# A decoder layer whose attention reads keys, queries and values from DRAM in padded rows

## The chip, the cores and the metric

The kernel runs on one core of one Trainium2 chip. The metric is the device time of one execution in microseconds (us); what is compared is the median of several executions. A profile is one execution taken by the hardware profiler. Its engines are PE (matmuls; their weight loads are listed apart as PEld), DVE, ACT and POOL (vector, scalar and general engines), and SP, which here only issues DMAs. "L702" is line 702 of the kernel before unless it is said to be of the kernel after.

## The reference, cut to what matters

x is 4 batches of 512 tokens of 256 features, float32. Three blocks follow one another, each with a residual:

```
x = x + mamba(layernorm(x))                 # two layers of a selective state space (SSM)
x = x + attention(layernorm(x), ctx_1024)   # 16 heads of 16, keys and values from ctx_1024
x = x + ffn(layernorm(x))                   # shared MLP and 8 experts, the best 2 of a token
```

The middle one is the one that the change is about:

```
q = h @ Wq.T + bq;  k = ctx @ Wk.T + bk;  v = ctx @ Wv.T + bv      # 4 batches, 512 x 256
p = softmax((q / 4) k^T)  per head of 16
return (p v) @ Wo.T + bo
```

A row of p sums to one, so bv adds the same vector to every row of p v, and bv @ Wo.T can be added to bo instead.

## The kernel before, in words

**SSM.** There are 8 steps (layer, batch), of 40 units each, in one loop over `units`. A unit with n > 0 treats one state of 256 channels over 512 tokens, as tiles of 128x1024: POOL multiplies m (L645), DVE scans v (L680) and h (L689), POOL multiplies h with Cs (L702), PE sums over the states into y (L716). Units with n = 0 come in halves of 128x512, whose first scan is done by PE as a product with a band (vf, L662). The order on every engine is the order in which the program is written. Besides its own work, a unit draws from two generators: `background`, which is the preparation of the next step (`prologue`), and `projections`, the output projection of the step before (po, L746, then the adds to the state xs and, in the second layer, of the layer's input, L755 and L757). In the last step nothing follows, and `background` is `kept_from`, which makes keys, values and queries for the attention: per batch it loads the context cT into one buffer, makes the queries of batches 0 to 2 (`queries`), the keys (pk, L820) and the values (pv, L841, with the bias bv as a matmul of a row of ones), and stores all three to DRAM as they are: 256 rows of 512. A line at the end of the unit decides whether `background` is advanced once or twice. When the loop ends, what is left of `kept_from` runs, then the last unit's sums, the gate z, and the last projection, that of batch 3.

**Start.** Before the loop the first step is prepared: projections (pp, L341), the short convolution (pc, L452, with the diagonal weights `taps` that POOL and others fill), dbc, rows of B and C that go through DRAM, ACT's w, ln and w (L539 to L544) in rotating buffers of one each, sums over time on PE (L524), and the copies of deltas and dxs that POOL's m needs.

**Attention.** Between the loop and the attention stand constants of the router and the loads of wg, wo, w1 (`up`), w2 (`dn`) and bo. Then the attention's own tiles are made: `kpad` and `qpad` have 4 groups of 4 heads, each head 32 partitions, of which 16 carry data; `fetched(b)` loads the data rows with 8 DMAs of 16 partitions x 4 x 512, and the rows between were filled once (zeros; in kpad a row of ones at 16, against which q carries the negative row maximum). `vpad` has 32 columns a head, 16 of them data, and a one. `fetched(b)` also loads v into a buffer, from which POOL copies it into vpad (L1251), and adds bo to the batch's state on POOL (L1252).

The attention has 16 units (batch, group) of 8 slots, again written out in order. PE works on scores twice: sc (L1329), whose row maxima DVE takes (L1335), and ten slots later (`LEAD`) sT with the maxima turned into q (`flipped`), which ACT exponentiates (L1340) and PE multiplies with vpad (L1278). sc and sT rotate through three PSUM buffers. The first ten slots hold only sc. Between the scores one generator, `between`, is advanced by a piece per slot: first the queries of batch 3, later `projected(b - 1)` (pn, pb and po on PE, L1203 adding po to xs on DVE) and `routed(b - 1)`, which chooses experts and ends in eight scatters issued by POOL (L1133). Where the third slot of a new batch is reached, all that is left of `between` is written out at once before the next one starts. The last batch's `projected` and `routed` run with the FFN, which needs them.

Of the kernel before, what the change touches and what calls it, by code (L numbers as in the profile page):

```python
# [17 lines left out]
P = 128  # L18
# [14 lines left out]
HS = 32  # L33
# [34 lines left out]
def decoder_layer(  # L68
# [73 lines left out]


    kept = ctx.enter_context(tc.tile_pool(name="kept", bufs=1, space=bass.MemoryType.DRAM))
    kept_k = [kept.tile([D, L], F32, name=f"kept_k{b}") for b in range(B)]
    kept_q = [kept.tile([D, L], F32, name=f"kept_q{b}") for b in range(B)]
    kept_v = [kept.tile([L, D], F32, name=f"kept_v{b}") for b in range(B)]

# [4 lines left out]
    def queries(b, bank, new, wqs, bqs):  # L153
# [27 lines left out]
        for m in range(KD):  # L181
# [7 lines left out]
            yield False  # L189
        nc.sync.dma_start(blocks(kept_q[b]), qs)  # L190
        yield False

    def chained(*steps):
        for s in steps:
            yield from s


    with ExitStack() as ph:
# [57 lines left out]
        def powers():  # L256
# [18 lines left out]
            nc.vector.memset(far[:NQ, 1], 0.0)  # L275

        def banded():

            for c in range(NCH):
                w = CHUNKS[c + 1] - CHUNKS[c]  # L280
                for r in range(NQ):
                    nc.scalar.activation(
                        band[:CR, c, r, :w], power[:CR, min(c, 1), :w], AF.Copy, scale=firsts[:CR, c, r : r + 1]
                    )
                yield
# [23 lines left out]
        def load_others(l):  # L309
            outw = wp.tile([P, NE, D], F32, name="outw")  # L310
# [279 lines left out]
        def gates_of(s):  # L590
            l, b = s
            if made[s][0] is None:
                made[s][0] = [pre2.tile([P, 2, L], F32, name="z") for _ in range(2)]
            return made[s][0]
# [53 lines left out]
        ys = {}  # L648
        projections = []

        filtering = {}
# [72 lines left out]
        def finished(s, e):  # L724

            l, b = s
            z = made[s][0]
            gated = z[e // 2][:, e % 2, :]
            nc.vector.tensor_tensor(gated, ys.pop((s, e)), gated, ALU.mult)
            if e < NE - 1:  # L730
                return
            made.pop(s)
            projections.append(projected(s, z))

# [31 lines left out]
        powers()  # L766
        load_others(0)
        while pairs[1] not in stored:
            next(background)
# [16 lines left out]
        def kept_from():  # L786
# [11 lines left out]
            nc.sync.dma_start(wv, blocks(wvT))  # L798
            vs = room[:, 2 * D : 6 * D].rearrange("p (t d) -> p t d", t=TB)
            bvs = room[:1, 6 * D : 7 * D]  # L800
            nc.sync.dma_start(bvs, bv.unsqueeze(0))
            ones = room[:1, 7 * D : 7 * D + P]
            nc.vector.memset(ones, 1.0)
            where = {"xn": "big", "xnT": "u", "qs": "w"}
            for b in range(B):
                cT = pre1.tile([P, KD, L], F32, tag="ln", name="cT")
                nc.sync.dma_start(cT, blocks(ctxT[b]))
                if b < B - 1:
# [8 lines left out]
                for m in range(KD):  # L817
# [10 lines left out]
                    nc.scalar.activation(ks[:, m, :], pk, AF.Identity, bias=bks[:, m : m + 1])  # L828
                nc.sync.dma_start(blocks(kept_k[b]), ks)
                for t in range(0, TB, 2):  # L830
                    pv = ps.tile([P, 2, D], F32, tag="mm", name="pv")
                    for i in range(2):
                        for k in range(KD):
                            nc.tensor.matmul(
                                pv[:, i, :],
                                cT[:, k, (t + i) * P : (t + i + 1) * P],
                                wv[:, k, :],
                                start=(k == 0),
                                stop=False,
                            )  # L840
                        nc.tensor.matmul(pv[:, i, :], ones, bvs, start=False, stop=True)  # L841
                    yield
                    nc.scalar.copy(vs[:, t : t + 2, :], pv)
                nc.sync.dma_start(blocks(kept_v[b]), vs)

        for u, (i, n, js) in enumerate(units):
# [87 lines left out]
        finished(*pairs[-1][:2])  # L934
        for _ in projections.pop():
            pass

# [5 lines left out]
    wgs = route.tile([P, KD, NX], F32, name="wgs")  # L943
    nc.sync.dma_start(wgs, blocks(wg))
    ties_to = route.tile([P, NX, NX], F32, name="ties_to")
# [51 lines left out]
    def behind(reader, writers):  # L997
# [17 lines left out]
    nc.vector.memset(counts[0], 0.0)  # L1015


    unit_row = route.tile([P, 1], F32, name="unit_row")
    nc.vector.tensor_reduce(
        unit_row, ident.rearrange("p (j r) -> p j r", r=HS)[:, :, HD : HD + 1].rearrange("p j o -> p o j"), AX.X, ALU.add  # L1020
    )

# [142 lines left out]
    wo = att_w.tile([P, KD, D], F32, name="wo")  # L1165
    nc.sync.dma_start(wo, blocks(woT))

    up = att_w.tile([P, KD, FF], F32, name="up")
    nc.sync.dma_start(up, blocks(w1))
    dn = att_w.tile([P, NF, D], F32, name="dn")  # L1170
    nc.sync.dma_start(dn, blocks(w2))
    bos = att_w.tile([P, D], F32, name="bos")
    nc.sync.dma_start(bos, bo.partition_broadcast(P))

# [31 lines left out]
    with ExitStack() as ph:  # L1206
# [5 lines left out]
        ph.enter_context(tc.manual_schedule())  # L1212

        qpads, kpads, vpads, tops = [], [], [], []
        for i in range(2):
            q = wp.tile([P, NG, L], F32, name=f"qpad{i}")
            nc.gpsimd.memset(q, 0.0)
            qpads.append(q)  # L1220
            k = wp.tile([P, NG, L], F32, name=f"kpad{i}")
            nc.vector.tensor_copy(
                k.rearrange("p g l -> p (g l)"), unit_row.to_broadcast([P, NG * L])
            )
            kpads.append(k)
        for i in range(2):
# [3 lines left out]
            tops.append(t)  # L1230

            v = wp.tile([P, TB, NH, HS], F32, name=f"vpad{i}")
            nc.vector.memset(v, 0.0)
            nc.gpsimd.memset(v[:, :, :, HD : HD + 1], 1.0)
            vpads.append(v)
# [6 lines left out]
        def fetched(b):  # L1242

            k, q = kpads[b % 2], qpads[b % 2]
            for dst, src in ((k, kept_k[b]), (q, kept_q[b])):
                rows = src.rearrange("(g j r) t -> j r g t", j=P // HS, r=HD)
                for j in range(P // HS):
                    nc.sync.dma_start(dst[j * HS : j * HS + HD], rows[j])
            v = ring.tile([P, TB, NH, HD], F32, tag="wide", name="v")
            nc.sync.dma_start(v.rearrange("p t h d -> p t (h d)"), blocks(kept_v[b]))  # L1250
            nc.gpsimd.tensor_copy(vpads[b % 2][:, :, :, :HD], v)  # L1251
            nc.gpsimd.tensor_tensor(  # L1252
                xs[:, b], xs[:, b], bos.unsqueeze(1).to_broadcast([P, TB, D]), ALU.add
            )

# [29 lines left out]

        fetched(0)
        held = None
        between = queries(B - 1, bank, lambda shape, name: ring.tile(shape, F32, tag="wide", name=name), wqs, bqs)
        un, outs, at = {}, {}, {}
        n = B * NG * 8  # L1290
        for s in range(-LEAD, n + 2):
# [3 lines left out]
            if k == 2 and g == 0 and 0 <= b < B:  # L1295
                un[b] = att_act.tile([P, NG, L], F32, name="un")
                if b > 0:
                    for _ in between:
                        held = None
                    between = chained(projected(b - 1, un[b - 1], bank), routed(b - 1, bank))  # L1300
            if k == 2 and g == 1 and b + 1 < B:
# [41 lines left out]

            if k == 6 and u + 1 < B * NG:
                held = flipped(u + 1)
# [14 lines left out]
        for _ in between:  # L1360
            pass


    with ExitStack() as ph:
        hold = ph.enter_context(tc.tile_pool(name="ffn_hold", bufs=1))
        act2 = ph.enter_context(tc.tile_pool(name="ffn_act2", bufs=2))
        act3 = ph.enter_context(tc.tile_pool(name="ffn_act3", bufs=3))
        act6 = ph.enter_context(tc.tile_pool(name="ffn_act6", bufs=6))
# [168 lines left out]
        def combined(b):  # L1537

            for c in range(TOP):
                first = NB * P + (c * B + b) * L  # L1540
                yt = act3.tile([P, TB, D], F32, name="yt")
                came = nc.sync.dma_start(yt, blocks(rows_out[first : first + L, :]))
# [16 lines left out]
def _arranged(i):  # L1559
# [28 lines left out]
        "wvT": i[c + "Wv"].T,  # L1588
        "bv": i[c + "bv"],
        "woT": i[c + "Wo"].T,  # L1590
# [24 lines left out]
```

## Time and profile before

| | |
|---|---|
| median of 3 runs | 1897.0 us (1896.61 to 1900.17) |
| profiled execution | 1896.35 us |
| its span, first to last instruction | 1894.7 us |
| mean granted clock of PE | 0.923 |
| busy: PE, DVE, ACT, POOL | 1619.6, 1388.7, 1045.4, 1245.6 us |
| SSM: last product of POOL ends | 1271.46 us |
| first sT of the attention | 1337.90 us |
| attention's last scatters, batch 2 | 1636.95 to 1646.99 us |
| L702 and L645 on POOL (192 each) | 2357 and 2358 ns |
| L680 and L689 on DVE (192 each) | 2281 and 2287 ns |

The times of the last rows are read from timelines and the chain of waits: an instruction's start and length in us from the span's start. The chain lists the work that ended last, piece by piece in order of time, each piece being what released the next; "issue" is time in which an engine waited for nothing that the profile shows. A waits line reads: engine and line that waited, what released it, then the sum in us, how often, and the longest. In a table by stretches, a pair such as 25.69 (x198) is an engine's busy time and its number of instructions there. The granted clock is the share of full speed that PE was given.

### The profile page before, as it was taken

The numbers are of one execution on the slowest core, as the hardware profiler recorded it, in microseconds if no ns is written. First come the engines' busy times: TensorE is split into PE (matmuls) and PEld (weight loads), VectorE is DVE, ScalarE is ACT, GpSimd is POOL, SyncE is SP. The second block draws the span as 40 slices with busy tenths as digits, with TensorE's granted clock in tenths as the row PEclk, the third lists the DMA queues.
The fourth block names the chain that finished last, engine by engine and source line by source line (L and its number), as shares of the span: only waits on it lengthen the run. The fifth ranks groups of instructions, "written<-read, shape, count | busy, mean of one in ns | idle before, by whom it ended". The sixth has DMA issues, their size and how long they took to land.

```text
span 1894.7 us, 28242 instructions
## 1 busy us (share of the span) xinstructions
PE 1619.6 (85%) x10714; PEld 751.3 (40%) x10714; DVE 1388.7 (73%) x1256; ACT 1045.4 (55%) x1635; POOL 1245.6 (66%) x782
## 2 busy tenths in 40 slices
PE   7779799799789889879879888785999999899995
PEld 2333343343343343334333343333333333466663
DVE  1388899889899889899898889975466676442223
ACT  3747668658677667667686765430454444412220
POOL 3488899899899889889889989972000201244540
PEclk9689899899889889899899899986899999999997
DMA  2433434435443343532543353414220200432214
GB/s 65 113 101 105 126 90 106 123 71 120 118 115 98 105 124 90 119 111 69 140 119 82 100 126 97 138 49 100 45 34 1 56 1 23 135 122 65 64 54 136
DMA packets 116120, 173.12 MB, mean 91 GB/s; under 512 B 18737, under 2 KB 57522, under 8 KB 115986
## 3 DMA queue, kind: packets, MB, share of 16 engines
q1 hardware_dynamic: 110706, 156.86, 32.0%
q0 software_dynamic: 5280, 14.46, 2.4%
q8 instruction: 85, 1.39, 0.3%
q14 instruction: 49, 0.40, 0.1%
HBM read 118.09 MB, written 53.17 MB: 90 GB/s over the span
## 4 chain that ended last, share of the span: by engine, by line
PE 52%; DVE 14%; ACT 12%; POOL 9%; issue 7%; DMA 5%; SPq 1%; POOLq 0%; DVEq 0%; ACTq 0%; another core or an unknown queue 0%
PE y L716 6%; PE sT L1329 5%; DVE v L680 5%; PE vf L662 4%; POOL h L702 4%; PE pc L452 4%; PE pw L1508 4%; PE pu L1485 4%; DVE h L689 3%; ACT decay L636 3%; PE o L1278 3%; PE pp L341 3%; PE sc L1329 3%; POOL m L645 2%; PE sum L524 2%
## 5 line engine op out<-in xcount | busy, mean ns | idle before, releaser
L702 POOL TENSOR_TENSOR h<-h,Cs 128x1024 f32<-128x1024 f32 x192 | 452.5, 2357 | 70.0 <-DVE h L689 61.7
L645 POOL TENSOR_TENSOR m<-dxs,Bs 128x1024 f32<-128x1024 f32 x192 | 452.6, 2358 | 23.8 <-DMA dxs<-wide 23.8
L689 DVE TENSOR_TENSOR_SCAN h<-decay,v 128x1024 f32<-128x1024 f32 x192 | 439.1, 2287 | 16.6 <-ACT decay L636 0.5
L680 DVE TENSOR_TENSOR_SCAN v<-beta,m 128x1024 f32<-128x1024 f32 x192 | 437.9, 2281 | 16.8 <-POOL m L645 12.7
L636 ACT ACTIVATE decay<-deltas,scaleA 128x511 f32<-128x511 f32 x512 | 333.1, 711 | 46.2 <-DVE h L689 38.2
L716 PE MATMUL y<-h,joined 128*32 128x512 f32 x768 | 218.0, 649 | 64.8 <-POOL h L702 64.8
L1335 DVE TENSOR_REDUCE tops<-sc 128x2 f32<-128x1024 f32 x128 | 156.4, 1225 | 103.9 <-PE sc L1329 96.8
L662 PE MATMUL vf<-band,dxT 106*32 106x102 f32 (+1 forms) x5120 | 188.4, 265 | 22.1 <-DVE hh L677 21.3
L1340 ACT ACTIVATE at<-sT 128x1024 f32<-128x1024 f32 x128 | 128.7, 1024 | 127.4 <-PE sc L1329 90.2
L677 DVE TENSOR_TENSOR_SCAN hh<-decay,vf 128x512 f32<-128x512 f32 x128 | 154.0, 1203 | 55.1 <-PE vf L662 42.8
L702 POOL TENSOR_TENSOR hh<-hh,Cs 128x512 f32<-128x512 f32 x128 | 163.4, 1276 | 43.2 <-DVE hh L677 40.7
L662 PEld LDWEIGHTS vf<-band,dxT 106*32 106x32 f32 (+1 forms) x5120 | 146.8, 114 | 104.6 <-issue 79.5
L1329 PE MATMUL sc<-kpad,qpad 32*128 32x512 f32 x512 | 149.7, 684 | 22.3 <-DMA qpad<-kept_q 17.0
L341 PE MATMUL pp<-xnT,inw 128*128 128x512 f32 x256 | 132.6, 649 | 6.2 <-ACT xnT L434 3.5
L1329 PE MATMUL sT<-q,kpad 32*128 32x512 f32 x512 | 135.9, 644 | 0.0
L452 PE MATMUL pc<-xpad,taps 128*128 128x512 f32 x256 | 118.6, 604 | 4.5 <-ACT xpad L446 4.5
L716 PEld LDWEIGHTS y<-h,joined 128*32 128x32 f32 x768 | 32.8, 114 | 161.7 <-POOL h L702 97.1
L113 POOL TENSOR_TENSOR rstd<-ve,neghalf 128x4 f32<-128x4 f32 x12 | 12.3, 1027 | 121.2 <-DVE ve L111 121.2
L636 ACT ACT_TABLE_LOAD x67 | 86.0, 1283 | 10.7 <-DVE h L689 9.3
L1517 POOL DMA_INDIRECT rows_out<-yg,target x39 | 40.0, 1027 | 75.8 <-DVE xgT L1478 64.8
L1133 POOL DMA_INDIRECT rows_in<-row,at x32 | 31.8, 993 | 81.2 <-DVE hit L1150 23.2
L341 PEld LDWEIGHTS pp<-xnT,inw 128*128 128x128 f32 x256 | 47.9, 202 | 79.5 <-issue 61.7
(249 smaller groups left out, 2359.5 us busy)
## 6 DMA issues: line engine op xcount, KB each, us to landing
deltas<-wide SPq DMA_DIRECT2D x256, 128.0 KB
dxs<-wide SPq DMA_DIRECT2D x256, 128.0 KB
rows_in<-nothing SPq DMA_DIRECT2D x17, 1028.0 KB
Cs<-rows SPq DMA_DIRECT2D x128, 64.0 KB
wide<-ln SPq DMA_DIRECT2D x16, 512.0 KB
wide<-w SPq DMA_DIRECT2D x16, 512.0 KB
Bs<-rows SPq DMA_DIRECT2D x32, 192.0 KB
xt<-in_x_dram SPq DMA_DIRECT2D x8, 512.0 KB
```

Source lines behind the costliest of these rows:

```text
L341: nc.tensor.matmul(pp, weights[l][1][half][:, k, m * P : (m + 1) * P], xnT[:, k, :], start=(k == 0), stop=(k == KD - 1),)
L452: nc.tensor.matmul(pcs[j], taps[:, e, k, :], xpads[j][:, k : k + L], start=(k == 0), stop=(k == KC - 1),)
L636: nc.scalar.activation(dA[:, j, 1:], copies[i][0][:, j, 1:], AF.Exp, scale=weights[s[0]][6][:, e, q + j, n : n + 1])
L645: nc.gpsimd.tensor_tensor(m, copies[i][1], Bs[:, n - 1, :].unsqueeze(1).to_broadcast([P, 2, L]), ALU.mult)
L662: nc.tensor.matmul(v[r * QP : (r + 1) * QP, CHUNKS[c] : CHUNKS[c + 1]], made[s][5][e // 2][:k, c, first : first + QP], band[:k, c, r, : CH ...
L677: nc.vector.tensor_tensor_scan(h, dA[:, 0, :], v, 0.0, ALU.mult, ALU.add)
L680: nc.vector.tensor_tensor_scan(v.rearrange("p n t -> p (n t)"), beta.rearrange("p n t -> p (n t)"), entering.pop(u).rearrange("p n t -> p ...
L689: nc.vector.tensor_tensor_scan(h.rearrange("p n t -> p (n t)"), dA.rearrange("p n t -> p (n t)"), v.rearrange("p n t -> p (n t)"), 0.0, AL ...
L702: nc.gpsimd.tensor_tensor(h, h, Cs[n].unsqueeze(1).to_broadcast([P, len(js), L]), ALU.mult)
L716: nc.tensor.matmul(ys[s, e][(q + j) * QP : (q + j + 1) * QP, :], joined, hcs[j], start=False, stop=(u % per == per - 1),)
L1329: nc.tensor.matmul(o, l, m, start=True, stop=True)
L1335: nc.vector.tensor_reduce(top[:, t2, 2 * h : 2 * h + 2, HD : HD + 1], sc, AX.X, ALU.max, negate=True)
```

## The change

- In DRAM, keys and queries now have the padded layout: 512 rows of 512, with 32 rows a head; values have 512 columns. `rows_between`, called before the first step's preparation goes on, fills a tile of 16 partitions with zeros and one row of ones, and writes it by 8 DMAs of 512 KB (16 heads x 16 rows x 512) into the rows between of every table. The tile has the buffer that ACT's first w takes later.
- A store of keys or queries becomes two DMAs (`to_heads`). Values are put by ACT into padded buffers (three in turn, filled once by POOL) and stored by four DMAs of 256 KB a batch.
- The matmul that added bv is gone; `biased` makes bv @ Wo.T beside the scores and adds it to bos. xs + bos is now written where a new batch begins, after what was left of `between`, and for batch 3 after the attention's loop.
- In the attention, the fills and the copy into vpad are gone, and `fetched(b)` is 8 DMAs of 128x512 and one of 1 MB. `fetched(0)` comes first; the weights of attention, router and FFN are loaded after it.
- The contexts cT are loaded two ahead, and in the last step of the SSM `background` is advanced twice in every unit with n > 0.
- The last step's projection is no longer run at the SSM's end: `completed` does it as the first piece of `between`. z and outw lie in pools that live on, and the FFN's yt takes their room.
- A `flipped(-1)` that the loop ran before the first unit, and whose result nothing used, is left out.

The core of the diff:

```diff
+        def rows_between():
+
+            blank = pre1.tile([P, 2, L], F32, tag="w", name="blank")
+            nc.gpsimd.memset(blank[:HD], 0.0)
+            nc.gpsimd.memset(blank[:1, 0, :], 1.0)
+            for i, tables in enumerate((kept_k, kept_q)):
+                for dst in tables:
+                    nc.sync.dma_start(
+                        dst.rearrange("(h r) t -> r h t", r=HS)[HD:],
+                        blank[:HD, i, :].unsqueeze(1).to_broadcast([HD, NH, L]),
+                    )
...
+    def to_heads(dst, src):
+
+        for m in range(KD):
+            n = P // HD
+            rows = dst[m * n * HS : (m + 1) * n * HS, :].rearrange("(h r) t -> h r t", r=HS)
+            nc.sync.dma_start(rows[:, :HD, :], src[:, m, :])
...
         load_others(0)
+        rows_between()
...
-                        nc.tensor.matmul(pv[:, i, :], ones, bvs, start=False, stop=True)
                     yield
-                    nc.scalar.copy(vs[:, t : t + 2, :], pv)
-                nc.sync.dma_start(blocks(kept_v[b]), vs)
+                    for i in range(2):
+                        at = vs[:, (b * TB + t + i) % 3]
+                        nc.scalar.copy(at[:, :, :HD], pv[:, i, :].rearrange("p (h d) -> p h d", d=HD))
+                        nc.sync.dma_start(
+                            kept_v[b][(t + i) * P : (t + i + 1) * P, :], at.rearrange("p h r -> p (h r)")
+                        )
+                if b + 2 < B:
+                    context(b + 2)
...
-                    n > 0 and (k == 0 and slot < 20 or units[(u + 1) % len(units)][1] > 0) or slot in (8, 23, 38)
+                    n > 0 and (k == 0 and slot < 20 or k == len(steps) - 1 or units[(u + 1) % len(units)][1] > 0) or slot in (8, 23, 38)
...
         finished(*pairs[-1][:2])
-        for _ in projections.pop():
-            pass
...
+        def fetched(b):
+
+            for g in range(NG):
+                for dst, src in ((kpads[b % 2], kept_k[b]), (qpads[b % 2], kept_q[b])):
+                    nc.sync.dma_start(dst[:, g, :], src[g * P : (g + 1) * P, :])
+            nc.sync.dma_start(vpads[b % 2].rearrange("p t h d -> p t (h d)"), blocks(kept_v[b]))
...
+        between = chained(
+            completed(),
+            queries(B - 1, bank, lambda shape, name: ring.tile(shape, F32, tag="wide", name=name), wqs, bqs),
+            biased(),
+        )
...
                 if b > 0:
                     for _ in between:
                         held = None
+                    nc.gpsimd.tensor_tensor(
+                        xs[:, b - 1], xs[:, b - 1], bos.unsqueeze(1).to_broadcast([P, TB, D]), ALU.add
+                    )
                     between = chained(projected(b - 1, un[b - 1], bank), routed(b - 1, bank))
...
         for _ in between:
             pass
+        nc.gpsimd.tensor_tensor(xs[:, B - 1], xs[:, B - 1], bos.unsqueeze(1).to_broadcast([P, TB, D]), ALU.add)
```

The two new functions of the attention:

```python
        def completed():

            z, outw = left
            cur = xs[:, B - 1]
            for t in range(TB):
                po = bank("po")
                for k in range(NE):
                    nc.tensor.matmul(
                        po[:, :D],
                        z[k // 2][:, k % 2, t * P : (t + 1) * P],
                        outw[:, k, :],
                        start=(k == 0),
                        stop=(k == NE - 1),
                    )
                yield True
                nc.vector.tensor_tensor(cur[:, t, :], cur[:, t, :], po[:, :D], ALU.add)
                if t == TB - 1:
                    nc.gpsimd.tensor_tensor(cur, cur, xt, ALU.add)
                yield False

        def biased():

            wide = ring.tile([P, KD, P], F32, name="wide_bv")
            nc.scalar.copy(wide, bvs.unsqueeze(2).to_broadcast([P, KD, P]))
            pb = bank("pb")
            for k in range(KD):
                nc.tensor.matmul(pb[:, :D], wide[:, k, :], wo[:, k, :], start=(k == 0), stop=(k == KD - 1))
            yield True
            nc.vector.tensor_tensor(bos, bos, pb[:, :D], ALU.add)
            yield False
```

More of the change, by code (lines that the diff above doesn't have):

```diff
@@ L144, in decoder_layer @@
     kept = ctx.enter_context(tc.tile_pool(name="kept", bufs=1, space=bass.MemoryType.DRAM))
-    kept_k = [kept.tile([D, L], F32, name=f"kept_k{b}") for b in range(B)]
-    kept_q = [kept.tile([D, L], F32, name=f"kept_q{b}") for b in range(B)]
-    kept_v = [kept.tile([L, D], F32, name=f"kept_v{b}") for b in range(B)]
+    kept_k = [kept.tile([NH * HS, L], F32, name=f"kept_k{b}") for b in range(B)]
+    kept_q = [kept.tile([NH * HS, L], F32, name=f"kept_q{b}") for b in range(B)]
+    kept_v = [kept.tile([L, NH * HS], F32, name=f"kept_v{b}") for b in range(B)]
+    def to_heads(dst, src):
[3 more added lines that the diff above has]
+            nc.sync.dma_start(rows[:, :HD, :], src[:, m, :])
     rows_in = kept.tile([NX * ROWS + SPARE * P, RW], F32, name="rows_in")
@@ L189, in queries @@
             yield False
-        nc.sync.dma_start(blocks(kept_q[b]), qs)
+        to_heads(kept_q[b], qs)
         yield False
@@ L195, in chained @@
             yield from s
+    late = ctx.enter_context(tc.tile_pool(name="late", bufs=1))
+    late2 = ctx.enter_context(tc.tile_pool(name="late2", bufs=2))
     with ExitStack() as ph:
@@ L309, in load_others @@
         def load_others(l):
-            outw = wp.tile([P, NE, D], F32, name="outw")
+            outw = late.tile([P, NE, D], F32, name="outw")
             nc.sync.dma_start(outw, blocks(out_wT[l]))
@@ L592, in gates_of @@
             if made[s][0] is None:
-                made[s][0] = [pre2.tile([P, 2, L], F32, name="z") for _ in range(2)]
+                made[s][0] = [late2.tile([P, 2, L], F32, name="z") for _ in range(2)]
             return made[s][0]
@@ L649, in decoder_layer @@
         projections = []
+        left = []
         filtering = {}
@@ L732, in finished @@
             made.pop(s)
-            projections.append(projected(s, z))
+            if s == steps[-1]:
+                left.extend((z, weights[l][5][0]))
+            else:
+                projections.append(projected(s, z))
         def projected(s, z):
@@ L798, in kept_from, with context @@
             nc.sync.dma_start(wv, blocks(wvT))
[L799 to L803, printed above, removed]
-            where = {"xn": "big", "xnT": "u", "qs": "w"}
+            vs = room[:, KD * D :].rearrange("p (i h r) -> p i h r", i=3, r=HS)
+            nc.gpsimd.memset(vs, 0.0)
+            nc.gpsimd.memset(vs[:, :, :, HD : HD + 1], 1.0)
+            where = {"xn": "big", "xnT": "u", "qs": "w"}
+            cTs = []
+            def context(b):
+                pool, tag = ((pre1, "ln"), (pre2, "Bs"), (pre1, "ln"), (pre2, "dxT"))[b]
+                cTs.append(pool.tile([P, KD, L], F32, tag=tag, name="cT"))
+                nc.sync.dma_start(cTs[b], blocks(ctxT[b]))
+            context(0)
+            context(1)
             for b in range(B):
-                cT = pre1.tile([P, KD, L], F32, tag="ln", name="cT")
-                nc.sync.dma_start(cT, blocks(ctxT[b]))
+                cT = cTs[b]
                 if b < B - 1:
@@ L828, in kept_from @@
                     nc.scalar.activation(ks[:, m, :], pk, AF.Identity, bias=bks[:, m : m + 1])
-                nc.sync.dma_start(blocks(kept_k[b]), ks)
+                to_heads(kept_k[b], ks)
                 for t in range(0, TB, 2):
@@ L838, in kept_from @@
                                 start=(k == 0),
-                                stop=False,
+                                stop=(k == KD - 1),
                             )
-                        nc.tensor.matmul(pv[:, i, :], ones, bvs, start=False, stop=True)
                     yield
-                    nc.scalar.copy(vs[:, t : t + 2, :], pv)
-                nc.sync.dma_start(blocks(kept_v[b]), vs)
+                    for i in range(2):
[6 more added lines that the diff above has]
+                    context(b + 2)
         for u, (i, n, js) in enumerate(units):
@@ L943, in decoder_layer @@
     wgs = route.tile([P, KD, NX], F32, name="wgs")
-    nc.sync.dma_start(wgs, blocks(wg))
     ties_to = route.tile([P, NX, NX], F32, name="ties_to")
@@ L1015, in decoder_layer @@
     nc.vector.memset(counts[0], 0.0)
[L1018 to L1021, printed above, removed]
     def routed(b, bank):
@@ L1165, in decoder_layer @@
     wo = att_w.tile([P, KD, D], F32, name="wo")
-    nc.sync.dma_start(wo, blocks(woT))
     up = att_w.tile([P, KD, FF], F32, name="up")
-    nc.sync.dma_start(up, blocks(w1))
     dn = att_w.tile([P, NF, D], F32, name="dn")
-    nc.sync.dma_start(dn, blocks(w2))
     bos = att_w.tile([P, D], F32, name="bos")
-    nc.sync.dma_start(bos, bo.partition_broadcast(P))
     def projected(b, un, bank, ts=range(TB)):
@@ L1212, in decoder_layer @@
         ph.enter_context(tc.manual_schedule())
[L1216 to L1225, printed above, removed]
+        qpads = [wp.tile([P, NG, L], F32, name=f"qpad{i}") for i in range(2)]
+        kpads = [wp.tile([P, NG, L], F32, name=f"kpad{i}") for i in range(2)]
+        vpads = [wp.tile([P, TB, NH, HS], F32, name=f"vpad{i}") for i in range(2)]
+        def fetched(b):
[3 more added lines that the diff above has]
+            nc.sync.dma_start(vpads[b % 2].rearrange("p t h d -> p t (h d)"), blocks(kept_v[b]))
+        fetched(0)
+        tops = []
         for i in range(2):
@@ L1230, in decoder_layer @@
             tops.append(t)
[L1232 to L1235, printed above, removed]
+        bvs = wp.tile([P, KD], F32, name="bvs")
+        nc.sync.dma_start(bvs, bv)
         wqs = wp.tile([P, KD, D], F32, name="wqs")
@@ L1239, in decoder_layer @@
         nc.sync.dma_start(bqs, bq)
-        nc.scalar.mul(bqs, bqs, QSCALE)
[L1242 to L1254, printed above, removed]
+        xt = ring.tile([P, TB, D], F32, tag="wide", name="xt")
+        nc.sync.dma_start(xt, blocks(x[B - 1]))
+        nc.sync.dma_start(wo, blocks(woT))
+        nc.sync.dma_start(bos, bo.partition_broadcast(P))
+        nc.sync.dma_start(wgs, blocks(wg))
+        nc.sync.dma_start(up, blocks(w1))
+        nc.sync.dma_start(dn, blocks(w2))
+        nc.scalar.mul(bqs, bqs, QSCALE)
         def bank(name):
@@ L1284, in values @@
                 )
-        fetched(0)
-        held = None
-        between = queries(B - 1, bank, lambda shape, name: ring.tile(shape, F32, tag="wide", name=name), wqs, bqs)
+        def completed():
+            z, outw = left
+            cur = xs[:, B - 1]
+            for t in range(TB):
+                po = bank("po")
+                for k in range(NE):
+                    nc.tensor.matmul(
+                        po[:, :D],
+                        z[k // 2][:, k % 2, t * P : (t + 1) * P],
+                        outw[:, k, :],
+                        start=(k == 0),
+                        stop=(k == NE - 1),
+                    )
+                yield True
+                nc.vector.tensor_tensor(cur[:, t, :], cur[:, t, :], po[:, :D], ALU.add)
+                if t == TB - 1:
+                    nc.gpsimd.tensor_tensor(cur, cur, xt, ALU.add)
+                yield False
+        def biased():
+            wide = ring.tile([P, KD, P], F32, name="wide_bv")
+            nc.scalar.copy(wide, bvs.unsqueeze(2).to_broadcast([P, KD, P]))
+            pb = bank("pb")
+            for k in range(KD):
+                nc.tensor.matmul(pb[:, :D], wide[:, k, :], wo[:, k, :], start=(k == 0), stop=(k == KD - 1))
+            yield True
+            nc.vector.tensor_tensor(bos, bos, pb[:, :D], ALU.add)
+            yield False
+        held = None
+        between = chained(
[3 more added lines that the diff above has]
+        )
         un, outs, at = {}, {}, {}
@@ L1299, in decoder_layer @@
                         held = None
+                    nc.gpsimd.tensor_tensor(
+                        xs[:, b - 1], xs[:, b - 1], bos.unsqueeze(1).to_broadcast([P, TB, D]), ALU.add
+                    )
                     between = chained(projected(b - 1, un[b - 1], bank), routed(b - 1, bank))
@@ L1341, in decoder_layer @@
                 at[u, kb, h] = a
-            if k == 6 and u + 1 < B * NG:
+            if k == 6 and 0 <= u + 1 < B * NG:
                 held = flipped(u + 1)
@@ L1366, in decoder_layer @@
         act2 = ph.enter_context(tc.tile_pool(name="ffn_act2", bufs=2))
-        act3 = ph.enter_context(tc.tile_pool(name="ffn_act3", bufs=3))
         act6 = ph.enter_context(tc.tile_pool(name="ffn_act6", bufs=6))
@@ L1540, in combined @@
                 first = NB * P + (c * B + b) * L
-                yt = act3.tile([P, TB, D], F32, name="yt")
+                pool, tag = ((late2, "z"), (late2, "z"), (late, "outw"))[(2 * b + c) % 3]
+                yt = pool.tile([P, TB, D], F32, tag=tag, name="yt")
                 came = nc.sync.dma_start(yt, blocks(rows_out[first : first + L, :]))
@@ L1588, in _arranged @@
         "wvT": i[c + "Wv"].T,
-        "bv": i[c + "bv"],
+        "bv": i[c + "bv"].reshape(-1, P).T,
         "woT": i[c + "Wo"].T,
```

## The prediction

> **What bounds the kernel now.** I read the page's busy table, slices and chain first; then, for each place the change touches, a table of busy time by stretches, the chain of waits, the waits by what ended them, and single-engine timelines.
>
> The stretches (columns: length, then busy time of PE, PE's loads, DVE, ACT, POOL, then granted clock, DMA share, GB/s):
>
> ```profile
> 1145.00:1175.00 30.00, 25.69 (x198) 10.23 (x202) 28.28 (x16) 19.29 (x27) 30.00 (x16) 0.89 0.27 74
> 1285.00:1310.00 25.00, 8.00 (x36) 6.54 (x35) 12.38 (x11) 0.52 (x2) 9.20 (x18) 0.71 0.71 162
> 1310.00:1337.00 27.00, 22.27 (x60) 8.70 (x58) 15.15 (x22) 3.24 (x6) 4.59 (x4) 0.50 0.05 12
> 1400.00:1500.00 100.00, 96.58 (x602) 34.65 (x602) 69.30 (x109) 47.47 (x54) 14.81 (x16) 0.98 0.25 43
> ```
>
> The recurrence (to 1271.5) is bound by POOL with DVE behind it, the attention (1337.9 to 1636) by PE; between them lies a transition in which nothing is full. Its chain:
>
> ```profile
> 1295.48 5.24 DMA dn<-in_w_dram
> ...
> 1300.79 8.36 DMA qpad<-kept_q
> 1309.14 0.30 issue
> 1309.45 4.21 PE sc L1329 x8
> ...
> 1334.12 3.78 PE pq L184 x4
> 1337.90 1.15 PE sT L1329 x2
> ```
>
> POOL's last product of the recurrence (L702) ends at 1271.46; call it H. To the first sT (the first scores of the attention proper) it is 1337.90 − 1271.46 = 66.4 us. The padded fetches are queued on SP behind the FFN's weights, and the waits say what that costs: PE's first score waits 17.0 us for qpad.
>
> ```profile
> PE sc L1329 <- DMA qpad<-kept_q: 17.0, 1, 17.0
> ```
>
> **Transition: gain.** In the changed kernel the fetches stand first on SP. kpad's first transfer waits for H, since its room is the recurrence's; the first score then needs two of 256 KB. A cT of the same 512 KB takes 4.66 us in the chain, so the first score is near H + 4.7. The prologue from first score to first sT took 1337.90 − 1309.45 = 28.45. It loses a useless pt and q (about 1.9); the state's last projection joins it (32 records, 7.17 us at L746, before one add on POOL of 2.4), but some steps of the last batch's queries, among them the 3.78 us of pq just ahead of the first sT, slide behind it. I keep 28.5: first sT at H + 33.2, a gain of 33.2 (bounds H + 28, H + 36).
>
> Given back inside the PE-bound part: the transposes of xn (8, about 1.0), a pq (1.9), the bias product (0.9), and about 2.5 for DVE, where the normalisation stands in order ahead of score maxima and waits for x and POOL. Together 6. Net gain 27 (22 to 32). [...]
>
> **Start: the blank rows.** Eight transfers of 512 KB (4.19 MB) leave 16 partitions for DRAM. POOL fills them after its seed (12.67) and DVE's scan (15.0), so data flows from 17.5. Ahead of 41.7 the queue is empty. What is behind: rows<-dbc (41.70) in SP's queue, and ACT's w at L539 (48.09), which takes the blank's room and so waits for all eight. No 16-partition read is in the trace; the nearest row is the padded fetch, whose 128 KB pieces go into 16 partitions each:
>
> ```profile
> 1298.00:1299.00 1.00, 0.00 (x0) 0.00 (x0) 1.00 (x1) 0.00 (x0) 1.00 (x1) 0.50 1.01 349
> 1346.00:1347.00 1.00, 1.00 (x12) 0.16 (x10) 1.00 (x2) 0.98 (x1) 0.00 (x0) 1.00 1.06 107
> 1348.00:1349.00 1.00, 1.00 (x8) 0.19 (x2) 0.73 (x1) 0.87 (x1) 0.00 (x0) 1.00 1.10 107
> ```
>
> All DMA engines are busy in all three, but 16 partitions get 107 GB/s where 128 get 349. [...] At 107, 4.19 MB need 39.2 us: to about 57. At the 305 GB/s of the early loads, 14 us: to 31.5, before anyone waits. I take the row. Then w starts at 57.4 instead of 48.09, and its chain (two exponent steps, sums, DVE's w at 55.96, wide, deltas, first m at 67.0) is late by 9.3, plus cold sums: **+11** (0 to 15). Once late, POOL's first m is late by as much and the recurrence moves whole. POOL's band taps behind the fill (+3.9) end before PE needs them.
>
> **Recurrence's last step.** POOL has no room (30.00 of 30), so the fill of the padded v buffers (128x1536, near 1.8) is paid. The 32 bias matmuls leave (−7.4 of PE), batch 3's keys and values (+8, formerly 1271 to 1284) move in ahead of H, and two background steps a unit stand in front of y and vf on PE. PE has about 3.3 us spare in 30. ACT's 16 small copies and the doubled v stores (1 MB against 0.5 at 74 GB/s) fit. **+4** (0 to 9).
>
> **Attention: a wait added.** x + bos now is POOL's, queued where the batch turns. There the eight scatters of the batch before have just been given to POOL, and DVE's first `xs += po` (L1203) waits for the sum. At the last turn:
>
> ```profile
> 1636.95 1.07 POOL L1133 DMA_INDIRECT rows_in<-row,at  x1 [16.83 <-DVE hit L1151]
> ...
> 1646.01 0.98 POOL L1133 DMA_INDIRECT rows_in<-row,at  x1 [0.30 <-issue]
> ```
>
> ```profile
> 1640.04 0.42 DVE L1203 TENSOR_TENSOR xs<-xs,po 128x256 f32<-128x256 f32 x1 [1.35 <-PE po L1201]
> ```
>
> The sum would end at 1646.99 + 2.36 = 1649.4; so the add moves from 1640.04 by **+9.3**, and L1203 lies on the chain to the FFN. Behind it on DVE wait the other tokens' adds and the normalisation. For batch 2 the scatters end at 1498.97, the sum would at 1501.3, the add was at 1496.98: DVE stalls 4.4, and PE soon after, since its scores rotate through three pairs that DVE's maxima free: 3 (0 to 4.4). For batch 3, 1576.98 + 2.35 against 1574.16, 5.2 of DVE, 3 (0 to 5.2). Batch 1 finds POOL idle: 0. Sum **+15**.
>
> Padded fetches are larger afterwards (3 MB a batch against 1.5) but come as full partitions and half a batch (37 us) ahead: 0. The dropped fills, v copies and memsets lay in the transition or beside PE: already in the 33. FFN's borrowed buffers keep their number: 0.
>
> **Sum.** −27 + 11 + 4 + 15 = +3 (rounding up for joints, +4). Against the profiled 1896.35 (span 1894.7) that gives 1900; the median is 1897.0, 0.65 above, so 1901.
>
> **Rivals.**
> 1. *The blank rows are free* (reading from 16 partitions isn't held as writing into them): 11 less, 1890, faster. For: no row shows a read, and the queue is empty to 41.7. Against: the fetch row. 0.2.
> 2. *The moved work fills the last step and the prologue:* recurrence +9, first sT at H + 36, net gain 22: 1901 + 5 + 5 = 1911. For: DVE 28.28 and POOL 30.00 of 30. It decides once batch 3's keys come later than H. 0.2.
> 3. *The scatters cover nothing:* DVE's stall is caught up in batches 2 and 3 (DVE is busy only 69.30 of 100), and the last one overlaps FFN matmuls: −8 to −15, 1888 to 1893, faster. Against: L1203 at 1640.90 and 1647.01 is on the chain. 0.12.
> 4. *The change does less than it says:* the fetch is still late, since H frees its room; first score at H + 12: 1908. 0.05.
>
> **Numbers.** The likeliest case, 0.43, gives 1901 with about ±6. A measurement tells 0.2% (3.8 us) from no change: faster below 1893.2, slower above 1900.8. Case 1 and 3 give faster 0.29; the rest is split by the sum's small excess: same 0.21, slower 0.50. For 8 in 10 the range reaches to case 1's and 2's outer parts: 1885 to 1914. Faster and slower hold most; the likeliest's own range is 1895 to 1907.
>
> **What would show it.** ACT's w (L539 before) starting near 57 behind the blank DMAs, with 107 GB/s from 17 to 57, and first m near 78; if w starts at 48, case 1. H later than 1271.5 by about 15. First sc about 5 us after H, first sT about 33 after. A POOL wait of 4 to 9 us in front of the first `xs += po` in batches 2, 3 and after the attention; no such wait is case 3. I am wrong if H moves by over 20, or if the prologue runs at full clock.

## The result and the profile after

The changed kernel takes 1904.97 us (median of 10 runs, 1901.1 to 1910.88), the one before 1898.4 (10 runs): ratio 1.0038, 95% interval 1.0020 to 1.0056, or +6.6 us where +4 was forecast. The profiled execution of after is the slowest of its ten (1910.88, span 1909.2), so its end is 14.5 us later than that of before, more than the medians. Part of that is its own: between the first units and the fourth step its recurrence falls back by 5 us, which the experiment with early sums, the same up to that point, does not show. Why it falls back is open. POOL's last product of the recurrence therefore ends 22.8 us later than in before (1294.28), in the experiment with early sums 17.05 later. The ledger below uses that experiment up to there.

The start. Two stretches of after (columns as in the prediction: length, busy time of PE, PE's loads, DVE, ACT, POOL, then granted clock, DMA share, GB/s), then ACT's steps from u to w:

```profile
22.00:27.00 5.00, 5.00 (x13) 2.21 (x12) 0.00 (x0) 0.78 (x2) 5.00 (x9) 1.00 0.91 98
52.00:57.00 5.00, 0.00 (x0) 0.00 (x0) 0.00 (x0) 0.00 (x0) 0.00 (x0) 0.56 0.92 99
```

```profile
46.85 1.06 ACT L543 ACTIVATE u<-u 128x1024 f32<-128x1024 f32 x1
61.39 1.06 ACT L563 ACTIVATE w<-u 128x1024 f32<-128x1024 f32 x1 [13.48 <-issue]
```

All engines stand at 52 to 57 while the blank rows go out at 99 GB/s; w starts 13.3 later than in before (48.09). The 13.48 is labelled "issue", that is, the view names no releaser; experiments 1 and 4 tell what it was.

The transition, in after's chain:

```profile
1291.94 2.35 POOL h L727
1294.29 0.02 issue
1294.30 0.32 SPq L1249
1294.62 0.05 issue
1294.67 3.28 DMA qpad<-kept_q
1297.95 0.09 issue
1298.04 2.09 PE sc L1384 x8
...
1320.11 1.97 issue
1322.08 1.22 PE sT L1384 x2
```

The first score comes 3.8 us after POOL's last product, the first sT 27.8 after; it was 66.4. The stretch from first score to first sT, the prologue, has a mean clock of 0.78, where 1310 to 1337 of before had 0.50. The second row is a part of it, with half of the last projection's products:

```profile
1298.00:1322.00 24.00, 19.44 (x76) 9.77 (x76) 15.77 (x25) 0.20 (x1) 2.36 (x2) 0.78 0.57 194
1305.00:1315.00 10.00, 8.68 (x45) 4.43 (x45) 6.13 (x8) 0.20 (x1) 2.34 (x1) 1.00 0.68 224
```

The added wait, from the groups of after (the add of po to xs on DVE; behind the second bar the idle time ahead of it and its releasers) and from POOL's timeline:

```profile
L1230 DVE TENSOR_TENSOR xs<-xs,po 128x256 f32<-128x256 f32 x16 | 6.5, 414 | 24.1 <-POOL xs L1417 10.4 <-POOL xs L1352 9.7 <-PE po L1228 4.0
```

```profile
1490.10 0.97 POOL L1164 DMA_INDIRECT rows_in<-row,at  x1 [0.30 <-issue]
1491.08 2.36 POOL L1352 TENSOR_TENSOR xs<-xs,bos 128x1024 f32<-128x1024 f32 x1
```

In before, no POOL wait stands ahead of that add (4.9 us for PE's po). The sum follows the last scatter without a gap, and three adds of DVE wait 20.1 us for it.

### The profile page after: what moved, and what is told of

Read it like the earlier page. It is cut to its first block, busy times and chain, and to the rows that moved or that the text cites. A ratio compares the mean times of both kernels' runs of the same rounds, so it can differ in the third digit from the quotient of the medians.

```text
span 1909.2 us, 28260 instructions
## 1 busy us (share of the span) xinstructions
PE 1617.0 (85%) x10682; PEld 752.9 (39%) x10682; DVE 1380.0 (72%) x1252; ACT 1045.1 (55%) x1644; POOL 1238.1 (65%) x777
## 5 line engine op out<-in xcount | busy, mean ns | idle before, releaser
L727 POOL TENSOR_TENSOR h<-h,Cs 128x1024 f32<-128x1024 f32 x192 | 452.0, 2354 | 72.4 <-DVE h L714 66.4
L705 DVE TENSOR_TENSOR_SCAN v<-beta,m 128x1024 f32<-128x1024 f32 x192 | 437.9, 2281 | 16.5 <-POOL m L669 12.5
L113 POOL TENSOR_TENSOR rstd<-ve,neghalf 128x4 f32<-128x4 f32 x12 | 12.3, 1026 | 209.7 <-DVE ve L111 209.7
```

Of the source, the lines that this page charges most:

```text
L705: nc.vector.tensor_tensor_scan(v.rearrange("p n t -> p (n t)"), beta.rearrange("p n t -> p (n t)"), entering.pop(u).rearrange("p n t -> p ...
L727: nc.gpsimd.tensor_tensor(h, h, Cs[n].unsqueeze(1).to_broadcast([P, len(js), L]), ALU.mult)
```

## The experiments

Each ratio is to the kernel before on the same chip and in the same hours; chips differ by up to 0.3% (medians of before from 1893.14 to 1898.4), so times of different chips are compared by their ratios.

**1. Wide blank rows.** The tile has 128 partitions, a one in every 16th of its first half, and each table gets two DMAs:

```diff
-                        dst.rearrange("(h r) t -> r h t", r=HS)[HD:],
-                        blank[:HD, i, :].unsqueeze(1).to_broadcast([HD, NH, L]),
+                            rows.rearrange("(h r) t -> h r t", r=HS)[:, HD:, :], blank[:, i, :]
```

> The changed kernel with one thing different: the blank rows leave 128 partitions (16 DMAs of 256 KB) instead of 16 (8 of 512 KB); same bytes, same place in the order, same room. Port theory: 4.19 MB move at some 300 GB/s, done by about 32 us, so ACT's first w starts at 48 again (it was 61.4), the first product on POOL at 67 (it was 82), and the time falls by 15 (13 to 20) against the changed kernel, to about 1890. Rival, bytes or DRAM writes are the limit, not the partitions: the blanks still end near 60 and the time stays at 1905. Rival, the start isn't on the path: w moves back but the time falls by under 5.

Measured: 1886.89, ratio 0.9967 (0.9955 to 0.9979), 0.71% below the changed kernel's 1.0038, some 13.5 us. w starts at once after u:

```profile
45.71 1.06 ACT L548 ACTIVATE u<-u 128x1024 f32<-128x1024 f32 x1
46.85 1.06 ACT L568 ACTIVATE w<-u 128x1024 f32<-128x1024 f32 x1
```

So the slow blank rows are the price of the start. The rate was not the expected one, though: 205 GB/s at a DMA share of 0.53, not some 300. What the expectation calls the port theory rests here on the prediction's rows alone, 107 GB/s for 16 partitions and 349 for 128; no run shows ports.

```profile
28.00:32.00 4.00, 4.00 (x11) 1.78 (x10) 0.00 (x0) 0.88 (x2) 0.00 (x0) 1.00 0.53 205
```

**2. Early sums.** At the turn to batch 1 POOL adds bos to all four batches; the later sums are gone:

```diff
+                    for b2 in range(B) if b == 1 else ():
+                        nc.gpsimd.tensor_tensor(
+                            xs[:, b2], xs[:, b2], bos.unsqueeze(1).to_broadcast([P, TB, D]), ALU.add
+                        )
```

> The changed kernel with one thing different: POOL's sums xs + bos of all four batches are written at the turn to batch 1, where POOL is idle, instead of each at the turn that needs it, behind the eight scatters. Scatter theory: DVE's waits for POOL of 9.7 in the attention and 10.4 after it go, the steps from the second q on lose their jumps of 6.0, 4.9 and 8.5, and the time falls by 16 to 20 against the changed kernel, to about 1887. Rival, the jumps come from the larger fetches (3 MB a batch): only the 8.5 after the loop goes, to about 1896. Rival, PE's slack and the FFN cover it: no change, 1905.

Measured: 1883.33, ratio 0.9951 (0.9937 to 0.9965), some 16.5 us below the changed kernel. The waits for POOL are gone:

```profile
L1230 DVE TENSOR_TENSOR xs<-xs,po 128x256 f32<-128x256 f32 x16 | 6.6, 413 | 5.4 <-PE po L1228 4.5 <-issue 0.9
```

At the turn to batch 2, from the q of its first unit to the next q, it takes 22.1 us here (1466.38 to 1488.51), 22.05 in before and 28.06 in after; at the turn to batch 3 it is 22.1, 22.2 and 27.0. The fetches are as large as in the changed kernel, so they are not what made the jumps.

**3. Both** (version 3 from here on).

> Both edits together: wide blank rows and the early sums. If the two costs are separate, they add: 15 + 18 = 33 less than the changed kernel, 1872 (1866 to 1878), faster than the kernel before by over 1%. If they share a wait, the sum falls short of the two single gains by several us.

Measured: 1865.58, ratio 0.9863 (0.9846 to 0.9881), and again, beside experiments 8 and 9, 1865.59, ratio 0.9859 (0.9838 to 0.9880). Below the changed kernel by 33 us, where the two single gains make 30. By the intervals the two agree: the costs are separate. This is the fastest version: 1.4% faster than before.

> The version with both edits once more, as the measure for the next two on the same chip: ratio to before 0.986 (0.984 to 0.989), and the transition as it was: first score 3 to 5 us after POOL's last product, first sT 27.7 after.

**4. A room of its own for the blank tile**, one of h's buffers, which nothing else needs until the first unit:

```diff
-            blank = pre1.tile([P, 2, L], F32, tag="w", name="blank")
+            blank = ring3.tile([P, 2, L], F32, tag="h", name="blank")
```

> The changed kernel with one thing different: the blank tile lies in a room of its own (one of the buffers of h, free until the first unit), so ACT's w has nothing to wait for; the 16-partition DMAs stay where they are in the queue. If only w's wait for the room costs, w starts at 48 and the time falls by 13 to 15. If the queue costs too, since the rows of B and C, the stores and the copies of deltas and dxs are queued behind blank rows that end at 60: w at 48 but the first product on POOL at about 75 instead of 82, a gain of 6 to 7. If the queue alone decides: no gain.

Measured: 1894.64, ratio 1.0012 (1.0003 to 1.0021): some 5 us below the changed kernel, give or take 4. w starts at 47.77, right after u. POOL's first product of a state with Cs is 7.5 later than in before, against 14.8. So a third to a half of the price is w's wait for the room. The rest is SP's queue, which its issues show (start, length):

```profile
42.42 4.57 SPq L500 DMA_DIRECT2D rows<-dbc  x1
58.96 1.71 SPq L504 DMA_DIRECT2D Bs<-rows  x4
64.89 0.38 SPq L577 DMA_DIRECT2D wide<-ln  x1
```

The rows of B and C go out behind the blank rows, and SP waits 11.9 us for them to land before it can load Bs. The copy of ln, which ACT had ready at 56.3, stands behind those loads and goes out at 64.89; in before it did at 57.31.

**5. How the DMA is laid out.** Early sums and wide blank rows, but the 16 rows of a head outermost and 8 or 4 heads within:

```diff
+                            rows.rearrange("(h r) t -> r h t", r=HS)[HD:], blank[: HD * 8, i, :]
```

> Early sums, and blank rows from 128 partitions again, but each DMA of 256 KB is laid out with the 16 rows of a head outermost (16 x 8 x 512) instead of the 8 heads (8 x 16 x 512). The wide version before it moved 203 GB/s with the DMA engines busy 0.52 of the time. Splitting theory: a DMA is dealt to the engines by its outermost dimension, so 8 gave half the engines; with 16 outermost the share is near 1 and the rate near 350 to 400 GB/s, done by about 29 us. Rival: the rate is set by writing 2 KB pieces to DRAM, and stays at 200. The time is the same either way, 1 us around the version with both edits (ratio to before 0.986), since both are done before 41 us.

Measured: 1871.97, ratio 0.9868 (0.9841 to 0.9894), the time of version 3. The rate:

```profile
26.00:30.00 4.00, 4.00 (x10) 1.72 (x10) 0.00 (x0) 1.34 (x3) 2.06 (x4) 1.00 1.01 341
```

128 partitions and 256 KB as in experiment 1, but 341 instead of 205 GB/s at a share of 1.01 instead of 0.53. That fits a dealing of the DMA to the engines by its outermost dimension; which engine took which part is not shown.

> As the one with 16 rows outermost, but from 64 partitions (32 DMAs of 128 KB, each 16 x 4 x 512), so that the splitting is the same and only the partitions differ. [...] If only the outermost dimension matters and the 98 GB/s of the change had another cause: as fast as 128 partitions.

Measured: one run of 1871.85. From 64 partitions, 16 outermost, the rate, then SP's issues of the 32 DMAs:

```profile
26.00:30.00 4.00, 4.00 (x11) 1.80 (x10) 0.00 (x0) 1.27 (x2) 2.16 (x4) 1.00 0.59 202
```

```profile
16.55 10.25 SPq L298 DMA_DIRECT2D kept_k<-blank  x16
26.84 10.23 SPq L298 DMA_DIRECT2D kept_q<-blank  x16
```

The rate is near half of the 341 from 128 partitions, as one that goes with the number of partitions would be, but the share is 0.59, and the issues give a plainer reason. SP issues one DMA of 128 KB every 0.64 us, which is 204 GB/s, the rate that was measured. The last issue ends at 37.07, and from 38 to 42 the DMA moves only 15 GB/s, less than one of the 128 KB in all, so nothing piles up behind SP. The run therefore shows the pace of the issues, and not what 64 partitions could do. With 16 partitions it is otherwise: there the engines are busy (0.91) and slow (98 / 0.91 = 108 GB/s at a full share, where 128 partitions have 341 / 1.01 = 338).

**6. The double advance taken back**, on version 3:

```diff
-                    n > 0 and (k == 0 and slot < 20 or k == len(steps) - 1 or units[(u + 1) % len(units)][1] > 0) or slot in (8, 23, 38)
+                    n > 0 and (k == 0 and slot < 20 or units[(u + 1) % len(units)][1] > 0) or slot in (8, 23, 38)
```

> The version with both edits (wide blank rows, early sums), with the double advance in the recurrence's last step taken back. Theory: the keys and values of batch 3 are made after the last unit again, ahead of y and z on PE, so the first score comes 8 to 13 us later after POOL's last product, while the last step itself gets back its 2 to 3 us: slower by 8 (5 to 12), ratio to before about 0.990. Rival: the double advance only crowds the last step; without it the same time or faster.

Measured: 1869.16, ratio 0.9864 (0.9842 to 0.9887), no difference from version 3. My theory failed. In the last step this run gains 1.9 us against before, where version 3 loses 2.5; POOL ends at 1266.65 against 1272.12. Batch 3's keys and values are still made ahead of that:

```profile
1260.50 1.98 PE L860 MATMUL pk<-cT,inw 128*128 128x512 f32 x4
1262.32 1.89 PE L874 MATMUL pv<-taps,cT 128*128 128x256 f32 x8
1264.14 1.05 PE L746 MATMUL y<-h,joined 128*32 128x512 f32 x4
1265.13 1.99 PE L874 MATMUL pv<-taps,cT 128*128 128x256 f32 x8
1267.05 1.05 PE L746 MATMUL y<-h,joined 128*32 128x512 f32 x4
1273.33 2.09 PE L1390 MATMUL sc<-kpad,qpad 32*128 32x512 f32 x8 [5.23 <-DMA kpad<-kept_k]
```

The first sT follows the last product after 31.5 us instead of 27.7, which takes back nearly all of the gain. In before, pk of batch 3 had waited for its cT (4.66 us from 1264.52) with PE's later work behind it; the likely cause of the earlier keys is therefore the cT loaded two ahead, which I did not try alone.

**7. The last projection at the recurrence's end again**, on version 3: `completed` is left out of `between` and `projected` runs after the loop.

> The version with both edits, with the last projection of the states run at the recurrence's end again instead of beside the scores. Theory: PE is what fills the prologue (23.7 of 27 us at clock 0.68), and the same 32 records are made either way, so the first score comes later by 5 to 8 and the prologue is shorter by nearly as much: slower by 2 (0 to 4). Rival: the projection was a full part of the gain, 7 us of PE taken off the path: slower by 6 to 9.

Measured: 1874.9, ratio 0.9887 (0.9868 to 0.9907), 0.25% above version 3, some 5 us, with intervals that overlap, so the times alone leave it open. By the trace it is more: the q of batch 2's first unit comes in version 3 (1449.91) 177.8 after POOL's last product, here (1457.53) 186.3, so 8.5. The first score waits for the fetch, and the fetch waits for POOL:

```profile
1271.25 1.92 PE y L746 x4
1273.16 8.26 PE po L776 x32
1281.42 0.02 issue
1281.45 0.70 DVE xs L785
1282.15 0.07 issue
1282.21 1.27 POOL xs L787
1283.49 0.02 issue
1283.50 2.62 DMA kpad<-kept_k
1286.12 0.96 issue
1287.08 2.09 PE sc L1386 x8
```

The projection held the room of kpad by its buffer for x, which neither of my theories had. By the trace the rival (6 to 9) is the nearer one. The prologue, now without the projection, took 28.7 us instead of 24.1 at a mean clock of 0.61, with the transposes of xn and pq ahead of the first sT as in before:

```profile
1287.00:1316.00 29.00, 21.10 (x64) 7.52 (x68) 14.30 (x21) 4.22 (x9) 1.23 (x2) 0.61 0.47 149
```

**8. The first fetch behind the weights**, on version 3 (`fetched(0)` after the load of dn).

> The version with both edits, with the first fetch of padded keys, queries and values queued behind the weights again (bvs, wqs, bqs, xt, wo, bos, wgs, up, dn). Queue theory: some 2.5 MB at 350 to 390 GB/s stand in front, so the first score comes 7 us later, and the time is up by 7 (4 to 9), ratio near 0.990. Rival: the weights' rooms are free before the recurrence ends, they load early, and nothing changes.

Measured: 1874.64, ratio 0.9906 (0.9887 to 0.9925), 9 us above version 3 on the same chip. The first score waits 11.03 us for kpad, and comes 13.0 after POOL's last product instead of 3.5:

```profile
1284.22 2.09 PE L1390 MATMUL sc<-kpad,qpad 32*128 32x512 f32 x8 [11.03 <-DMA kpad<-kept_k]
```

**9. The kernel before with that order alone** (wo, wg, w1, w2 after the first fetch).

> The kernel before with one part of the change: wo, wg, w1 and w2 are loaded after the first fetch instead of ahead of it. Fill theory: in the kernel before the fetch has to wait for its room to be filled (DVE's copy into kpad ends at 1297.6) and moves 16 partitions at 107 GB/s, so the order alone brings 1 to 3 us, ratio 0.999; the change's gain needs the padded layout. Rival: the weights were what the 17 us wait for qpad was made of; 8 to 11 us less, ratio 0.995.

Measured: 1890.87, ratio 0.9987 (0.9977 to 0.9997), 2.5 us less. The order brings 9 us with the padded layout and 2.5 without it. There the fetch has to wait until DVE has filled kpad (its copy ends at 1297.29, and the first score comes at 1305.15), and it moves 16 partitions at a time.

## Why the prediction was right

An offset is how much later than in before the same piece of work comes.

| step | predicted | measured | where |
|---|---|---|---|
| start | +11 | +14.5 | first steps' offset with early sums; experiments 1, 4 |
| last step of the recurrence | +4 | +2.5 | offsets 14.56 to 17.05 with early sums |
| last product to first sT | −33.2 | −38.6 | 66.4 to 27.8 |
| first sT to the second unit's q | +6 | +8.1 | 15.7 to 23.8 |
| turns to batches 2 and 3 | +6 | +10.9 | 22.05 to 28.06, 22.2 to 27.0 |
| end of the attention | +9.3 | +8.5 | last add, less the offset of the last o (3.2) |
| sum | +3 | +5.9 | medians: +6.6 |

The signs were right in all six, and so were the main mechanisms: slow blank rows, an early fetch, sums behind scatters. That the sum came so near is in part luck: single terms missed by up to 5 us, and the errors point both ways.

- **Start.** The mechanism was right. The term mis-sized is the rate, 98 against 107 GB/s (4.19 MB in 42.7 instead of 39.2 us). The sums that I called cold came: the eight on PE behind w take 6.29 us at a clock of 0.61 (64.86 to 71.00), where before has 4.39 at 0.85 (51.60 to 56.00). w's wait, on which I worked the sum out, sets the price in the changed kernel, but it hides a second one: without it the queue alone still makes POOL 7.5 late (experiment 4).
- **Last step.** Experiments 1 and 3 have the same 2.5. I gave PE 3.3 us to spare in 30; the row that I showed leaves it 4.3. POOL's last product came 17.05 later with early sums. In the profiled execution of after it came 22.8 later, past the 20 that I had named as a sign of being wrong, by the 5 us that are that execution's own. What I held the double advance for, making room for batch 3's keys ahead of the last product, it did not do (experiment 6).
- **Transition.** The fetch was as predicted (first score 3.8 after against 4.7; queue order 9 us, experiment 8). The prologue took 24.0 instead of 28.5, and 3.8 us of pq that stood ahead of the first sT slid behind it and came back in the next line, 8.1 instead of 6. Both together: −30.5 against −27. From the first score to the second unit's q it is 44.2 us in before, 47.9 in after, and 44.2 again in experiment 7, which has no projection there. So the projection's 32 products, 8.9 us of PE, cost 3.7 us in that stretch; I had taken them for free and counted 6 for other pieces. The 28.5 took the clock to stay at before's row, 0.50 from 1310 to 1337, where PE was busy all of 1310 to 1320 and got no more. After speaks against that: 0.78 on average, and full speed from 1305 to 1315. That is between the row and the full clock that I had named as a sign of being wrong. Which share of the shorter prologue is the clock and which is pq is not separated.
- **Batch turns.** I had let PE's slack take 1.4 of DVE's 4.4 and 2.2 of its 5.2; it took next to nothing (6.0 and 4.9). The first add of batch 2 did move by 4.4, from 1489.1 (1496.98 less the offset) to 1493.47; the 1.6 that the turn took beyond that are not explained. In the row of before PE is 96.6 us busy of 100, which left little slack to count on.
- **End.** 9.3 predicted for the first add, 9.0 measured, 8.5 for the last.

Of the rivals, free blank rows and a covered stall are refuted by experiments 1 and 2. A full last step did not come: it took 2.5, and the first sT came 27.8 after, not 36. The late fetch is refuted by the chain. (The low end of the covered stall should have read 1886, which is 1901 − 15.)

## What to carry to other kernels

Look at what an engine has been given just before a moved instruction: one sum of 2.4 us behind eight scatters of 1.3 us cost 19 us in three places, and moving its line gained 16.5. A constant that is written to DRAM in the idle start is not free if its tile or its queue is needed before it ends (w came 13.3 late here, and with a room of its own for the tile POOL's first product with Cs still 7.5); make the transfer keep all DMA engines busy, and from more than 16 partitions (98 GB/s from 16 at a share of 0.91, 341 from 128 at 1.01). A change with a gain of 30 us in one place can lose it all in two others, and each has its own place in the trace.

## What the runs showed that I had not expected

- From the same 128 partitions, with the same 256 KB a DMA, the order of its dimensions alone made 205 GB/s at a DMA share of 0.53 (8 outermost) or 341 at 1.01 (16 outermost).
- A share near 1 doesn't mean a full rate: 16 partitions keep the DMA engines 0.91 busy at 98 GB/s. And half the rate doesn't mean half the partitions: small DMAs (128 KB) went out no faster than SP issued them, one every 0.64 us.
- A busy PE doesn't have to be a fast one. In before it was busy for 10 us without a gap, on scores of 32 rows and four transposes, at half the clock; what the clock goes by is not shown.

```profile
1310.00:1320.00 10.00, 10.00 (x30) 4.35 (x30) 6.76 (x10) 0.00 (x0) 3.35 (x2) 0.50 0.12 31
```

- The room of a tile, not data, decided the first fetch twice: POOL's last product frees kpad's in the changed kernel, the sum with x does when the projection is at the end (12.3 us later, 1283.50 against 1271.20).
